# A selective-scan and attention kernel: preparing images 3 and 4 beside attention, taking shared buffers together, and a denser share of products on TensorE

## The chip, the cores and the metric

The kernel runs on one core of a Trainium2 chip. Its engines work side by side, each through its own queue in order: PE (TensorE, matrix products), DVE (VectorE), ACT (ScalarE, activation functions and copies), POOL (GpSimd), and SP (SyncE), which here only issues DMAs. The metric is the device time of one execution in microseconds (us), less is better.

## The reference

Four images of 384 channels and 32x32 positions go through a selective-scan layer, causal attention and a mixture of four experts. Everything is float32. Shortened:

```
x = x + conv(_gn(x), ...)                  # group norm in front
  # conv: xs = the image in 4 directions (rows, columns, both reversed)
  x_dbl = einsum('bkdl,kcd->bkcl', xs, x_proj_weight)   # -> dts (12), Bs (16), Cs (16)
  dt = softplus(einsum('bkrl,kdr->bkdl', dts, dt_projs_weight) + dt_projs_bias)
  def step(h, inp):                        # scan over 1024 positions
      dA = exp(dtt[..., None] * A)
      h = h * dA + (dtt * ut)[..., None] * bt[:, :, None, :]
      y = einsum('bkdn,bkn->bkd', h, ct)
  ys = ys + Ds * u ; merge the 4 directions ; layer norm ; exact gelu
t = tokens(x)                              # 1024 tokens of 384
t = t + attn(_ln_t(t), Wq, Wk, Wv)         # one head of 384, causal softmax
t = t + ffn(_ln_t(t), ...)                 # best 2 of 4 experts kept, 384 -> 1536 -> 384
```

## The kernel before

**Units.** The scan of an image is cut into 192 units, 768 in all. A unit is a tile of 128 partitions (32 channels by 4 states) and 1024 positions. For each unit ACT makes the decay `da` (L552, exp), DVE the input `v` = `du` x B (L559, `front`) and the scan `h` (L565, `middle`), POOL the product `h` x C (L572, `back`), and after every four units PE sums over states into `y` (L597, `row`). `back` of a unit is ordered behind `front` of the next one, so that POOL's product runs beside a scan and not beside a product of DVE. `da` has three buffers, so ACT can be two units ahead at most.

**`v` by PE, image 0 only.** In the first image PE has little else to do. For some groups of four units the side program `feed` lets PE turn `du` (`turn`, L815), ACT scales the turned tile by B (32 small activations per group, L838, into `st`), and PE turns it back into `v` (L860, `turned`), so that DVE doesn't make that product. Before, these are the groups with odd `q`, where time permits.

**Preparation.** `preparation(b)` loads an image, takes the group norm, projects it (`project_x`), and for each of 3 channel blocks and 2 pairs of directions runs `project_dt`: two halves of matmuls `pdt` (L425), softplus on ACT (L431), a DMA of `dt` to memory, the product `du` (L439) on DVE and its DMA. The scan fetches both from memory, a few units ahead. Exp and softplus need different function tables on ACT, so that each change between `da` and `dt` loads a table. One preparation runs at a time; `yield "wait", n` lets n steps pass.

**What follows the scan.** After an image's last unit its sum is evicted (L617), layer-normed and gated (`finish`), and `behind(b)` runs its attention and experts beside the scan of the next image, from the list `waiting`, one image at a time. The last image's run alone after the last unit. In the scores' softmax (L1012 to L1018) DVE takes the minimum of each block, of two blocks at L1016, and ACT the exponential.

**Order of the work.** All of it is written out by hand, by a clock that advances one step per unit. In each step the main loop puts down, in this order: `decay` of two units ahead, deferred work, `front`, `turned`, `back`, inner work such as the softmax, `middle`, `row`, fetches, one piece of the running preparation, and then `go_on`, which steps side programs and the head of `waiting`. `go_on` has a budget of PE time per step, `pace`: PACE_A (4.4) in attention and PACE_E in the experts; each generator says with `yield "pe", n` what it used. Because every engine works in order, a place in this sequence is a place in each queue.

**Shared buffers.** Eight SBUF slots of 4 KB per partition (`slots`) and four PSUM banks (`banks`) are handed out by `Shared`. Expert weights, `dt` and `du` tiles, attention's weights and probabilities and the squares of layer norms all live in slots; `take` waits until one is free, step by step.

Of the kernel before, what the change touches and what calls it, by code (L numbers as in the profile page):

```python
# [9 lines left out]
AF = mybir.ActivationFunctionType  # L10
ALU = mybir.AluOpType
# [4 lines left out]
P = 128  # L16
B = 4
C = 384
M = C // P
HW = 32  # L20
L = HW * HW
# [12 lines left out]
NQ = N // NI  # L34
NJ = P // DJ
# [7 lines left out]
AHEAD = 5  # L43
SLOTS = 8
PACE_A = 4.4
PACE_E = 3.3


@with_exitstack
def hybrid_kernel(  # L50
# [22 lines left out]
    nc = tc.nc  # L73
# [37 lines left out]
    clock = [-100]  # L111
# [6 lines left out]
    class Shared:  # L118
# [15 lines left out]
        def take(self, name, *shape):  # L134
            while not self.ready():
                yield "wait", 1
            return self.now(name, *shape)

        def give(self, *names):
            for name in names:  # L140
# [268 lines left out]
    def project_dt(b, pair, m, u, xd):  # L409

        ks = PAIRS[pair]
        while not slots.ready(3 + pair):
            yield "wait", 1
        v = u[m]
        if pair == 1:
            v = slots.now(f"ut_{b}_{m}", P, L)
            nc.scalar.copy(v.rearrange("p (w h) -> p w h", h=HW), columns(u[m]))
        dts = [slots.now(f"dt_{b}_{k}_{m}", P, L) for k in ks]
        for h in range(NH):
            while not banks.ready(2):  # L420
                yield "wait", 1
            pss = [banks.now(f"pdt_{b}_{k}_{m}_{h}") for k in ks]
            for i, k in enumerate(ks):
                r = slice(64 * pair + 32 * i, 64 * pair + 32 * i + R)
                nc.tensor.matmul(  # L425
                    pss[i], wdt[r, m * P : (m + 1) * P], xd[r, bass.ts(h, 512)],
                    start=True, stop=True,
                )
            yield "wait", 1
            for i, k in enumerate(ks):  # L430
                nc.scalar.activation(  # L431
                    dts[i][:, bass.ts(h, 512)], pss[i], AF.Softplus, bias=dtb[:, k, m : m + 1]
                )
                banks.give(f"pdt_{b}_{k}_{m}_{h}")
        yield "wait", 1
        for i, k in enumerate(ks):
            nc.sync.dma_start(dts_d[b, k][0, m * P : (m + 1) * P, :], dts[i])
            du = yield from slots.take(f"du_{b}_{k}_{m}", P, L)
            nc.vector.tensor_mul(du, dts[i], v)  # L439
            yield "wait", 1  # L440
            nc.sync.dma_start(dts_d[b, k][1, m * P : (m + 1) * P, :], du)
            if b == 0:
                stored_du.add((k, m))
            slots.give(f"dt_{b}_{k}_{m}", f"du_{b}_{k}_{m}")
        if pair == 1:
            slots.give(f"ut_{b}_{m}")

    EACH = NQ * NJ
    IMAGE = M * K * EACH
# [30 lines left out]

    def preparation(b):

        u = first_x if b == 0 else load_image(b)
        yield "wait", 3
        yield from groupnorm(b, u)
        while clock[0] < IMAGE * (b - 1) + 24:

            yield "wait", 1
        xd = one.tile([P, L], F32, tag="xd", name=f"xd_{b}")
        if b == 0:  # L490
            nc.scalar.activation(dump, eps, AF.Softplus)
            scan_weights()
        yield from project_x(b, 0, u, xd)
        if b == 0:
            fetch(-3, ("bc",))
            first_dt(u, xd)
            yield "start", 0
        yield from project_x(b, 1, u, xd)
        for m in range(M):
            for pair in range(2):  # L500
                if b > 0 or m > 0 or pair > 0:
                    yield from project_dt(b, pair, m, u, xd)
                yield "wait", 0 if b == 0 and m == 0 else 12

    units = [
        dict(b=b, pair=pair, i=i, k=k, m=m, q=q, j=j, name=f"{b}_{m}_{k}_{q}_{j}")
# [120 lines left out]
    def layernorm(dst, src, name, lag):  # L627

        width = src.shape[2]
        n = width // 512
        mus = []
        for h in range(n):
            mu = yield from banks.take(f"mu_{name}_{h}")
            for c in range(M):
                nc.tensor.matmul(  # L640
                    mu, mean_w, src[:, c, bass.ts(h, 512)], start=(c == 0), stop=(c == M - 1)
                )
            mus.append(mu)
            yield "pe", 2.6
        yield "inner", 0
        for h in range(n):
            s = bass.ts(h, 512)
            nc.vector.tensor_tensor(
                dst[:, :, s], src[:, :, s], mus[h].unsqueeze(1).to_broadcast([P, M, 512]),
                ALU.subtract,  # L650
            )
            banks.give(f"mu_{name}_{h}")
        sqs = []
        for c in range(M):
            sq = yield from slots.take(f"sq_{name}_{c}", P, width)
            sqs.append(sq)
        for h in range(n):
            for c in range(M):
                s = bass.ts(h, 512)
                nc.scalar.activation(sqs[c][:, s], dst[:, c, s], AF.Square)  # L660
        yield "wait", lag
        var = yield from banks.take(f"var_{name}")
        for h in range(n):
            for c in range(M):
                for q in range(4):
                    o = h * 512 + q * P
                    nc.tensor.matmul(
                        var[32 * q : 32 * (q + 1), h * P : (h + 1) * P], mean_w[:, :32],
                        sqs[c][:, o : o + P], start=(c == 0), stop=(c == M - 1),
                        tile_position=(0, 32 * q),  # L670
                    )
            yield "pe", 1.0
        slots.give(*[f"sq_{name}_{c}" for c in range(M)])
        rs = one.tile([P, n, P], F32, tag=f"rs{n}", name=f"rs_{name}")
        nc.scalar.activation(
            rs, var[:, : n * P].rearrange("p (h t) -> p h t", t=P), AF.Sqrt, bias=eps
        )
        banks.give(f"var_{name}")
        yield "wait", 1
        nc.vector.reciprocal(rs, rs)  # L680
        yield "wait", lag
        backs = []
        for h in range(n):
            spread_ = yield from banks.take(f"rb_{name}_{h}")
            for q in range(4):
                nc.tensor.matmul(  # L686
                    spread_[:, q * P : (q + 1) * P],
                    ident[:, 32 * q : 32 * q + 1].to_broadcast([P, P]), rs[:, h, :],
                    start=True, stop=True,
                )  # L690
# [85 lines left out]
    def feed():  # L776
# [21 lines left out]
        for n in range(0, IMAGE, EACH):  # L798
# [16 lines left out]
                    nc.tensor.transpose(ps[:, t * P : (t + 1) * P], du[:, o : o + P], ident)  # L815
                return ps

            for q in range(1, NQ, 2):
                n0 = n + q * NJ
                if clock[0] > n0 - AHEAD:  # L820
                    continue
                while len(begun) >= 2 and clock[0] < begun[-2] + NJ:

# [61 lines left out]

            defer(1 + m // 2, add)

    def scaled_tokens(b, yb):

        sqs = []  # L890
        for c in range(M):
            sq = yield from slots.take(f"sq_at_{b}_{c}", P, L)
            nc.scalar.activation(sq, yb[:, c, :], AF.Square)
            sqs.append(sq)

        var = yield from banks.take(f"var_at_{b}")
        for o, src in ((NH * P, [yb[:, c, :] for c in range(M)]), (0, sqs)):
# [10 lines left out]
        slots.give(*[f"sq_at_{b}_{c}" for c in range(M)])  # L908
        rs = one.tile([P, NH, P], F32, tag=f"rs{NH}", name=f"rs_at_{b}")
        flat = rs.rearrange("p h t -> p (h t)")  # L910
        nc.scalar.activation(flat, var[:, NH * P : 2 * NH * P], AF.Square)
        yield "inner", 0
        nc.vector.tensor_tensor(flat, var[:, : NH * P], flat, ALU.subtract)
# [28 lines left out]
    def attention(b, yb, fx0):  # L942
# [2 lines left out]
        while not folded:  # L945
            yield "wait", 1
        gw_ = []
        for name, w in ((f"wg_{b}", g_d), (f"wv_{b}", wv_d)):
            ta = yield from slots.take(f"{name}a", P, 2, C)
            nc.sync.dma_start(ta, w[:, :2, :])  # L950
            tb = yield from slots.take(f"{name}b", P, C)
            nc.sync.dma_start(tb, w[:, 2, :])
            gw_.append((ta[:, 0, :], ta[:, 1, :], tb))
        xn = yield from scaled_tokens(b, yb)
        qt = pools["ht"].tile([P, M, L], F32, tag="ht", name=f"qt_{b}")
        vt = pools["ht"].tile([P, L // P, C], F32, tag="ht", name=f"vt_{b}")

# [50 lines left out]
        def softmax(i, ss, pr):  # L1008
# [4 lines left out]
            for n, (o, e, ps) in enumerate(ss):  # L1013
                nc.vector.tensor_reduce(nb[:, n : n + 1], ps, AX.X, ALU.min)  # L1014
            if len(ss) == 2:
                nc.vector.tensor_tensor(nb[:, 0:1], nb[:, 0:1], nb[:, 1:2], ALU.min)  # L1016
            for n, (o, e, ps) in enumerate(ss):
                nc.scalar.activation(  # L1018
                    pr[:, o:e], ps, AF.Exp, bias=nb[:, 0:1], scale=-1.0,
# [5 lines left out]
        def normalise(i, nb, n):  # L1025
            wd = (i + 1) * P
            if n == 2:
                nc.vector.tensor_add(nb[:, 2:3], nb[:, 2:3], nb[:, 3:4])
            nc.vector.reciprocal(nb[:, 2:3], nb[:, 2:3])
            nc.scalar.activation(prs[i][:, :wd], prs[i][:, :wd], AF.Copy, scale=nb[:, 2:3])  # L1030

# [445 lines left out]
```

## Time and profile before

| | us |
|---|---|
| median of 3 runs | 3781.38 (3779.78 to 3781.87) |
| profiled execution | 3782.19 |
| its span | 3780.4 |

```profile
PE 3348.6 (89%) x11755; PEld 1523.6 (40%) x11755; DVE 2962.4 (78%) x2098; ACT 2088.0 (55%) x2754; POOL 1815.4 (48%) x776
...
L565 DVE TENSOR_TENSOR_SCAN h<-da,v 128x1024 f32<-128x1024 f32 x768 | 1750.6, 2284 | 107.2 <-PE v L860 31.8
L552 ACT ACTIVATE da<-dt,a 128x1024 f32<-128x1024 f32 x768 | 882.8, 1156 | 916.0 <-DVE h L565 877.8
L559 DVE TENSOR_TENSOR v<-du,bc 128x1024 f32<-128x1024 f32 x678 | 840.6, 1240 | 35.0 <-DMA du<-dts 18.3
```

The first line gives each engine's busy time, its share of the span and its instructions. In the others stand line, engine, operation, output and inputs, shape and count, then busy us and mean ns of one, then the idle time of the engine just before such instructions and what ended most of it. The shares are averages over stages that differ: image 0 has no attention or experts beside it, and after the last unit there is no scan.

### The profile page before, as it was taken

How to read it: one execution, taken by the hardware profiler on the slowest of the kernel's cores; microseconds unless marked ns; L12 is line 12 of the kernel's file. 1: busy time of each engine (PE TensorE's matmuls, PEld its weight loads, DVE VectorE, ACT ScalarE, POOL GpSimd, SP SyncE). 2: the span in 40 equal slices, each digit the busy share in tenths (PEclk: the TensorE clock that was granted, in tenths of full speed). 3: DMA queues.
4: the chain of work that ended last, by engine and by line, in shares of the span. 5: the costliest groups of instructions: out<-in, count | busy, mean ns of one | idle time of the engine just before them, and what ended most of it. 6: DMA issues, size and time to landing. Idle time of an engine off the chain costs nothing. (4 is left out here: it accounts for less than half of the span.)

```text
span 3780.4 us, 34707 instructions
## 1 busy us (share of the span) xinstructions
PE 3348.6 (89%) x11755; PEld 1523.6 (40%) x11755; DVE 2962.4 (78%) x2098; ACT 2088.0 (55%) x2754; POOL 1815.4 (48%) x776
## 2 busy tenths in 40 slices
PE   4666666689999999799999999889999998999999
PEld 1333323345343334345333344454344334644444
DVE  5899899988899899989988999999999992210000
ACT  5888888555666556556655555455554552322121
POOL 2777777545466556545555565455665660000000
PEclk7777876799999999898999999899999999999999
DMA  6656555635676757436666655455667551322321
GB/s 202 221 211 223 203 210 200 235 141 177 211 247 210 253 197 245 152 136 219 218 218 227 203 201 197 143 172 196 209 197 241 178 182 38 91 78 81 97 82 53
DMA packets 408017, 680.01 MB, mean 180 GB/s; under 512 B 33520, under 2 KB 279968, under 8 KB 407840
## 3 DMA queue, kind: packets, MB, share of 16 engines
q1 hardware_dynamic: 401632, 677.40, 52.6%
q8 instruction: 93, 1.52, 0.2%
q10 hardware_dynamic: 6208, 0.39, 0.1%
q14 instruction: 84, 0.69, 0.1%
HBM read 605.16 MB, written 72.55 MB: 179 GB/s over the span
## 5 line engine op out<-in xcount | busy, mean ns | idle before, releaser
L572 POOL TENSOR_TENSOR h<-h,bc 128x1024 f32<-128x1024 f32 x768 | 1814.3, 2367 | 1300.8 <-DVE v L559 1170.4
L565 DVE TENSOR_TENSOR_SCAN h<-da,v 128x1024 f32<-128x1024 f32 x768 | 1750.6, 2284 | 107.2 <-PE v L860 31.8
L552 ACT ACTIVATE da<-dt,a 128x1024 f32<-128x1024 f32 x768 | 882.8, 1156 | 916.0 <-DVE h L565 877.8
L1260 PE MATMUL ph<-fx,w 128*128 128x512 f32 x2304 | 1023.3, 600 | 3.5 <-DMA w<-in_w 2.0
L1285 PE MATMUL fy<-ht,w 128*128 128x512 f32 x2304 | 1022.4, 601 | 1.7 <-ACT dt L431 0.9
L559 DVE TENSOR_TENSOR v<-du,bc 128x1024 f32<-128x1024 f32 x678 | 840.6, 1240 | 35.0 <-DMA du<-dts 18.3
L1285 PEld LDWEIGHTS fy<-ht,w 128*128 128x128 f32 x2304 | 437.1, 192 | 575.9 <-issue 558.9
L1260 PEld LDWEIGHTS ph<-fx,w 128*128 128x128 f32 x2304 | 433.8, 191 | 578.6 <-issue 532.8
L597 PE MATMUL y<-h,sel 128*32 128x512 f32 x3072 | 489.7, 659 | 97.4 <-POOL h L572 97.2
L1245 ACT ACTIVATE ht<-ph,b1s 128x512 f32<-128x512 f32 x384 | 257.5, 678 | 463.3 <-PE ph L1260 462.5
L1294 DVE SCALAR_TENSOR_TENSOR fy<-fy,b2s,tw 128x512 f32<-128x512 f32 x96 | 72.4, 754 | 423.0 <-PE fy L1285 423.0
L597 PEld LDWEIGHTS y<-h,sel 128*32 128x32 f32 x3072 | 97.6, 116 | 407.4 <-issue 219.0
L860 PE MATMUL v<-ident,st 128*128 128x128 f32 x720 | 144.2, 366 | 112.7 <-DVE h L565 111.6
L838 ACT ACTIVATE st<-turn,bt 128x128 f32<-128x128 f32 x736 | 213.6, 532 | 0.1
L860 PEld LDWEIGHTS v<-ident,st 128*128 128x128 f32 x720 | 116.1, 190 | 158.3 <-DVE h L565 77.9
L1249 ACT ACTIVATE ht<-ht 128x3072 f32<-128x3072 f32 x64 | 176.9, 2764 | 0.8
L552 ACT ACT_TABLE_LOAD x108 | 138.6, 1283 | 15.5 <-DMA dt<-dts 11.8
L1067 PE MATMUL po<-pt,vt 128*128 128x256 f32 x480 | 110.2, 383 | 10.1 <-ACT pt L959 10.0
L425 PE MATMUL pdt<-xd,wdt 12*128 12x512 f32 x184 | 78.9, 753 | 33.4 <-ACT dt L431 24.7
L997 PE MATMUL ss<-axn,qt 128*128 128x512 f32 (+3 forms) x288 | 101.3, 497 | 7.7 <-ACT yb L1084 6.4
L1067 PEld LDWEIGHTS po<-pt,vt 128*128 128x128 f32 x480 | 96.0, 204 | 27.8 <-ACT pt L959 13.1
L997 PEld LDWEIGHTS ss<-axn,qt 128*128 128x128 f32 x288 | 50.5, 193 | 50.2 <-issue 30.0
(208 smaller groups left out, 1618.3 us busy)
## 6 DMA issues: line engine op xcount, KB each, us to landing
bc<-rows SPq DMA_DIRECT2D x384, 512.0 KB, 4.7
w<-in_w SPq DMA_DIRECT2D x384, 384.0 KB, 5.9
dt<-dts SPq DMA_DIRECT2D x192, 512.0 KB, 3.9
du<-dts SPq DMA_DIRECT2D x192, 512.0 KB, 6.5
dts<-dt SPq DMA_DIRECT2D x48, 512.0 KB, 3.6
dts<-du SPq DMA_DIRECT2D x48, 512.0 KB, 3.8
fx<-t2d SPq DMA_DIRECT2D x12, 768.0 KB, 5.8
tw<-mkd SPq DMA_DIRECT2D x32, 256.0 KB, 6.5
```

Source lines behind the costliest of these rows:

```text
L552: nc.scalar.activation(u["da"], spread["dt4", n], AF.Exp, scale=a4[:, g, u["q"] : u["q"] + 1])
L559: return nc.vector.tensor_tensor(u["v"], spread["du4", n], spread["bc", n][:, 0, :], ALU.mult)
L565: nc.vector.tensor_tensor_scan(u["h"][:, ::step], u["da"][:, ::step], u["v"][:, ::step], 0.0, op0=ALU.mult, op1=ALU.add,)
L572: product = nc.gpsimd.tensor_tensor(h, h, spread["bc", n][:, 1, :], ALU.mult)
L597: nc.tensor.matmul(y, sel, h, start=first, stop=last, tile_position=(0, jj * DJ))
L838: nc.scalar.activation(st[:, 4 * h + t, :].rearrange("p (d i) -> p i d", i=NI)[:, i, :], ps[h][:, t * P : (t + 1) * P], AF.Copy, scale=bt[ ...
L860: nc.tensor.transpose(u["v"][:, t * P : (t + 1) * P], st[:, t, u["j"] * P : (u["j"] + 1) * P], ident)
L1067: nc.tensor.matmul(pv[:, o:], vt[:, j, m * P : (m + 1) * P], pts[step][j // 4][:, j % 4, o:], start=(alone and j == 0), stop=(j == nj - 1),)
L1245: nc.scalar.activation(ht[:, f, :], ps, AF.Identity, bias=bias)
L1249: nc.scalar.activation(ht, ht, AF.Gelu)
L1260: nc.tensor.matmul(ps, tiles[n][:, c, (f % 2) * P : (f % 2 + 1) * P], xns[h][:, c, :], start=(c == 0), stop=(c == M - 1),)
L1285: nc.tensor.matmul(pss[m], tiles[n][:, f, :], hts[fh][:, f, :], start=(fh == 0 and f == 0), stop=(fh == 1 and f == FH - 1),)
```

## The change

- `PACE_E` goes from 3.3 to 3.45.
- `together` takes several slots at once when all are free; the squares of the layer norms use it.
- In `project_dt` the wait between the first and the second half's matmuls and activations is left out for the second half as long as the first image is scanned.
- `preparation` of images 2 and 3 (counted from 0) starts at most 30 steps before the image in front of them is scanned, their projections start with that image instead of 24 steps later, and the pauses between projections become 4 steps for image 1 and 1 step for images 2 and 3, where they were 12.
- In `feed` the groups that PE makes are those whose number leaves 1, 3 or 4 when divided by 5, instead of the odd ones.
- Attention fetches its weights into slots after its squares are given back, instead of before.
- Two operations on one number per partition in the softmax are `tensor_scalar` instead of `tensor_tensor`.

```diff
-PACE_E = 3.3
+PACE_E = 3.45
@@ class Shared
+        def together(self, names, *shape):
+            while not self.ready(len(names)):
+                yield "wait", 1
+            return [self.now(name, *shape) for name in names]
@@ project_dt
-            yield "wait", 1
+            if h == 0 or clock[0] >= IMAGE:
+                yield "wait", 1
@@ preparation
+        while b > 1 and clock[0] < IMAGE * (b - 1) - 30:
+            yield "wait", 1
         u = first_x if b == 0 else load_image(b)
...
-        while clock[0] < IMAGE * (b - 1) + 24:
+        while clock[0] < IMAGE * (b - 1):
             yield "wait", 1
...
-                yield "wait", 0 if b == 0 and m == 0 else 12
+                yield "wait", (0 if m == 0 else 12, 4, 1, 1)[b]
@@ layernorm
-        sqs = []
-        for c in range(M):
-            sq = yield from slots.take(f"sq_{name}_{c}", P, width)
-            sqs.append(sq)
+        sqs = yield from slots.together([f"sq_{name}_{c}" for c in range(M)], P, width)
@@ feed
-            for q in range(1, NQ, 2):
+            for q in range(NQ):
                 n0 = n + q * NJ
-                if clock[0] > n0 - AHEAD:
+                if n0 // NJ % 5 not in (1, 3, 4) or clock[0] > n0 - AHEAD:
                     continue
@@ scaled_tokens(b, yb, between)
+        sqs = yield from slots.together([f"sq_at_{b}_{c}" for c in range(M)], P, L)
         for c in range(M):
-            sq = yield from slots.take(f"sq_at_{b}_{c}", P, L)
-            nc.scalar.activation(sq, yb[:, c, :], AF.Square)
-            sqs.append(sq)
+            nc.scalar.activation(sqs[c], yb[:, c, :], AF.Square)
...
         slots.give(*[f"sq_at_{b}_{c}" for c in range(M)])
...
+        while not slots.ready(4):
+            yield "wait", 1
+        between()
@@ attention
-        for name, w in ((f"wg_{b}", g_d), (f"wv_{b}", wv_d)):
-            ta = yield from slots.take(f"{name}a", P, 2, C)
...
-        xn = yield from scaled_tokens(b, yb)
+        def weights():
+            for name, w in ((f"wg_{b}", g_d), (f"wv_{b}", wv_d)):
+                ta = slots.now(f"{name}a", P, 2, C)
...
+        xn = yield from scaled_tokens(b, yb, weights)
@@ scores
-                nc.vector.tensor_tensor(nb[:, 0:1], nb[:, 0:1], nb[:, 1:2], ALU.min)
+                nc.vector.tensor_scalar_min(nb[:, 0:1], nb[:, 0:1], nb[:, 1:2])
@@ normalise
-                nc.vector.tensor_add(nb[:, 2:3], nb[:, 2:3], nb[:, 3:4])
+                nc.vector.tensor_scalar_add(nb[:, 2:3], nb[:, 2:3], nb[:, 3:4])
```

More of the change, by code (lines that the diff above doesn't have):

```diff
@@ L886, in finish, with scaled_tokens @@
             defer(1 + m // 2, add)
-    def scaled_tokens(b, yb):
-        sqs = []
+    def scaled_tokens(b, yb, between):
+        sqs = yield from slots.together([f"sq_at_{b}_{c}" for c in range(M)], P, L)
         for c in range(M):
-            sq = yield from slots.take(f"sq_at_{b}_{c}", P, L)
-            nc.scalar.activation(sq, yb[:, c, :], AF.Square)
-            sqs.append(sq)
+            nc.scalar.activation(sqs[c], yb[:, c, :], AF.Square)
         var = yield from banks.take(f"var_at_{b}")
@@ L947, in attention @@
         gw_ = []
-        for name, w in ((f"wg_{b}", g_d), (f"wv_{b}", wv_d)):
-            ta = yield from slots.take(f"{name}a", P, 2, C)
[L950 to L953, printed above, removed]
-        xn = yield from scaled_tokens(b, yb)
+        def weights():
+            for name, w in ((f"wg_{b}", g_d), (f"wv_{b}", wv_d)):
+                ta = slots.now(f"{name}a", P, 2, C)
+                nc.sync.dma_start(ta, w[:, :2, :])
+                tb = slots.now(f"{name}b", P, C)
+                nc.sync.dma_start(tb, w[:, 2, :])
+                gw_.append((ta[:, 0, :], ta[:, 1, :], tb))
+        xn = yield from scaled_tokens(b, yb, weights)
         qt = pools["ht"].tile([P, M, L], F32, tag="ht", name=f"qt_{b}")
```

## The prediction

> **What bounds the kernel now.** I read the windows first, cut where the scans of units 0, 192, 384, 576 begin (the view of tile `h` gives 50.3, 682.9, 1511.4 and 2331.6), at the end of the last scan (3114.3) and where the last image's projections begin (3177).
>
> ```profile
> core 0: us, PE busy (x) PEld busy (x) DVE busy (x) ACT busy (x) POOL busy (x), PEclk, DMA share, GB/s
> 50.30:682.90 632.60, 394.61 (x1806) 192.61 (x1806) 582.57 (x327) 517.62 (x1047) 454.72 (x191) 0.72 0.61 216
> 682.90:1511.40 828.50, 772.58 (x2781) 347.98 (x2782) 765.08 (x543) 502.41 (x547) 452.55 (x192) 0.96 0.60 210
> 1511.40:2331.60 820.20, 773.59 (x2654) 335.36 (x2653) 762.65 (x526) 470.65 (x496) 452.34 (x192) 0.96 0.58 200
> 2331.60:3114.30 782.70, 743.25 (x2596) 327.10 (x2595) 748.90 (x512) 416.71 (x442) 452.22 (x192) 0.97 0.56 188
> 3114.30:3177.00 62.70, 50.00 (x275) 26.27 (x274) 21.75 (x20) 18.92 (x20) 2.47 (x2) 0.88 0.17 57
> 3177.00:3780.00 603.00, 594.27 (x1590) 284.38 (x1590) 65.88 (x131) 147.99 (x189) 0.00 (x0) 1.00 0.26 76
> ```
>
> The scans set the pace: DVE is busy for 92 to 96% of each of the first four windows. In image 0 ACT is next (82%), in the other images PE (93 to 95%). After 3177 PE alone matters; the chain of waits runs there through `ph` and `fy` with no gaps, so nothing in the change can shorten those 603 us. What DVE waits for in images 1 to 3, and in image 0:
>
> ```profile
> DVE nb L1014 <- PE ss L1002: 22.6, 6, 10.8
> DVE du L439 <- PE ph L1260: 16.8, 3, 10.0
> DVE du L439 <- PE fy L1285: 13.9, 4, 7.7
> ...
> DVE du L439 <- ACT dt L431: 3.3, 3, 1.9
> ...
> DVE h L565 <- PE v L860: 31.8, 22, 3.8
> ```
>
> The `du` product of a preparation waits for its delta projection, which stands in PE's queue behind expert matmuls: 35 us with the smaller rows (1.0 for `da`), 19 of them in image 1, 16 in image 2. The last line is image 0's: nearly every group of four whose `v` PE makes ends in a wait of about 1.45 us.
>
> One row is out of proportion, a minimum over two numbers per partition:
>
> ```profile
> L1016 DVE TENSOR_TENSOR nb<-nb x16: 159/1303/1712, 825.8 to 3242.5; 128x1 f32<-128x1 f32 x16
> 862.47 2.34 POOL L572 TENSOR_TENSOR h<-h,bc 128x1024 f32<-128x1024 f32 x1 [1.86 <-DVE v L559]
> 863.53 1.30 DVE L1016 TENSOR_TENSOR nb<-nb 128x1 f32<-128x1 f32 x1
> 864.75 2.27 DVE L565 TENSOR_TENSOR_SCAN h<-da,v 128x1024 f32<-128x1024 f32 x1
> L341 DVE TENSOR_SCALAR gn_vc<-gn_vc x3: 154/155/155, 358.7 to 1407.5; 128x3 f32<-128x3 f32 x3
> ```
>
> It starts inside POOL's product (862.47 to 864.81) and ends with it. In the last image, with POOL silent, it takes 0.16.
>
> Where the scans end, experts of image 2 are still in PE's queue and hold up the last image:
>
> ```profile
> 3112.04 2.29 DVE L565 TENSOR_TENSOR_SCAN h<-da,v 128x1024 f32<-128x1024 f32 x1
> 3125.65 1.28 DVE L617 SCALAR_TENSOR_TENSOR yb<-xe,dsum,y 128x1024 f32<-128x1024 f32 x1 [11.32 <-PE y L597]
> 3133.54 1.75 DVE L648 TENSOR_TENSOR yb<-yb,mu_l 128x1536 f32<-128x1536 f32 x1 [6.61 <-PE mu_l L640]
> ```
>
> [...] 1.30 us beside POOL, 0.16 without. [...] For three elements the trace shows no such wait (0.155 us at L341, 0.23 at L340, POOL running); for one element no run here shows it. [...] a load from 1017.79 is followed by its softplus at 1019.08. I price a switch at 1.28.
>
> **The change part by part.**
>
> *Minimum by `tensor_scalar`.* 12 of the 16 minima lie among scans, at 1.37 us mean, four per image from 1 to 3. At 0.16 to 0.24 each, 4 x 1.2 = 5 us per image, on DVE and just ahead of a scan. Bounds: 0 [...] and 15 in all. The adds at L1028 take 0.13 already: nothing.
>
> *Which groups PE makes (`q` loop).* The orders of both programs give 208 instead of 184 transposes into `turn` and 824 instead of 720 into `v`, that is 103 units instead of 90. DVE loses 13 products of 1.24 plus a 0.06 gap: -17 us. Two more `du` fall into image 0 (those that image 1 has after unit 192 now): +2.6. In the new pattern two such groups often stand in a row. ACT gets 96 more scalings at 0.30 (8 took 2.42): +28; and as both halves of a projection are now activated together before unit 192, 11 pairs of table loads go: -28. Two more projections and the third image's statistics also enter: +20. So ACT has about 537 us of work for some 620, and the projections of image 1, spread over units 110 to 204 before, now stand at 105 to 159, where ACT's work comes to 3.2 to 3.3 us a unit against DVE's 3.0 to 3.4. I take 1.45 us of wait for each of the three further groups and 3 us for that crowding: -14.4 + 7.3 = -7. Bounds: -20 (waits go with the table loads) and +8 (ACT sets the pace in units 96 to 168).
>
> *Preparations beside attention.* Image 2's projections move from units 238 to 335 to units 192 to 233, image 3's from 408 to 504 to 384 to 426; their 2 x 12 `du` stay, and so do their PE and ACT work and their DMAs (12 loads of `x` and stores of `xn`, rows and dts: their data are needed 150 units later). The `du` waits among experts go: -19 and -16. In the new place they stand behind PE's `pq` and `pv`, where DVE already waits 5.3 and 10.8 us (`nb` L1014), and ACT gets about 8.7 us per projection (half a 1.98 copy, four 0.65 softplus, four loads of 1.28). Counted from the changed program's order with the durations of before, ACT comes to 3.3 to 4.4 us per unit there, DVE to 4.4 to 5.1, so DVE still leads on the average; in-order queues will cost something: I take +8 per image. Bounds 0 and +30. Image 1 also loses 2 `du` (-2.6).
>
> *`together`, and weights fetched after the squares (`between`).* Same allocations and DMAs, other moments. SP's landing time for such transfers is 4 to 7 us and three more steps of attention follow before `pq`: 0, covered by the normalisation; if not, under 7 us per image.
>
> *PACE_E 3.45.* An expert counts 12 x 2.6 + 6 x 5.1 = 61.8: 18.7 units before, 17.9 after. PE needs 144 x 0.427 = 61.5 us for it plus about 0.48 us of `y` per unit (16 matmuls, 1.92 us, every fourth unit): 70.5 before, 70.1 after. DVE at 3.62 a unit (scan, product, gaps) plus three times 1.44 for `fy`: 72 before, 69.5 after. PE becomes the bound by about 0.6 us per expert: +3 in image 1, +1 in image 2 (its preparation is gone from there), +5 in image 3, where also 2 to 3 more `fy` pairs come in front of the last scan (+3).
> In return image 2's experts end at step 769 instead of 779 of the kernel's clock (its scheduling rules followed through); the last scan is 767. Before, from the scan's end to `pq` are 62.7 us. Without experts in between: POOL 2.4, `y` 1.9, a PE lag of 3, eviction 1.3, means 5.3, subtraction 1.8, squares 1.7, variance 1.5, root and reciprocal 2.2, spreading and product 5: about 26 to the end of L696; from there to `pq` the trace has 20.2 (3156.75 to 3177). 46 to 49 instead of 62.7: -14. Bounds -18 and -4 (PE lags by a whole expert).
>
> Sum: image 0 -7; image 1: -5 - 2.6 - 19 + 8 + 3 = -15; image 2: -5 - 16 + 8 + 1 = -12; image 3: -5 + 3 + 5 = +3; tail -14. Together -45. The profiled execution took 3782.2 (span 3780.4 and 1.8 around it), 0.8 above the median of 3781.4: 3737.
>
> **The rivals.** *All waits go* (attention takes the projections for nothing, image 0 keeps its full 14): -45 - 16 - 7 = -68, with lower waits at L860 about -78: 3704. For it: DVE leads in every stage by the sums. Against: PE and ACT work in order and would be busy for 80 to 97%. *Attention gives most of it back:* the du waits reappear there at some 3 us each projection more: 3772. For it: those 10.8 us waits at L1014. *Slower: a moved wait.* The 12 projections meet `pq`, `pv` and the softmax in PE's and ACT's queues, and each `du` holds every scan behind it. The two worst such waits now are 7.7 and 10.0; at 8 us for each projection the attention parts lose 96 instead of the 16 I allow: -45 + 80 = +35, 3817. It decides the sign from 5 us per projection on. Against it: PE is busy only 180.5 of 219.3 us in 682.9 to 902.2, while the waits now come from stretches where it is full. *The change doesn't take hold:* minima still blocked (+15) and PE late among experts (+15 more): 3767.
>
> **How the numbers follow.** Forecast (3720 to 3757) 0.60, all waits go 0.14, given back or not taking hold 0.16, slower 0.10. The range, 3702 to 3772, takes in all but the slower case and the ends of the others. Faster than the 0.2% (7.6 us) that a measurement can tell from no change: 0.86, within it 0.04, slower 0.10.
>
> **What would show it.** L1026 (the minimum) at 0.2 us; no `du` waits behind `ph` or `fy`, and below 25 us behind others; 103 units by PE and image 0 near 625 us; `nb` waits of 30 us or less; 46 to 50 us from the last scan to `pq`; PE at 97% among experts. It is wrong if image 0 is longer than 633, if attention stretches lengthen by over 30 us each beyond their added `du`, or if expert units take over 4.0 us.

## The result and the profile after

| | before | after |
|---|---|---|
| median of 8 runs each, us | 3781.28 (3779.78 to 3784.8) | 3769.9 (3768.69 to 3772.26) |
| ratio | | 0.9968 (0.9959 to 0.9978) |
| span of the profiled execution | 3780.4 | 3770.5 |

The change makes the kernel 11.4 us faster, a quarter of the 44 forecast. The page of the changed kernel, with the engines' line, the scan and the product `v`:

```profile
PE 3354.8 (89%) x11883; PEld 1539.0 (41%) x11883; DVE 2951.9 (78%) x2085; ACT 2084.8 (55%) x2832; POOL 1817.5 (48%) x776
...
L574 DVE TENSOR_TENSOR_SCAN h<-da,v 128x1024 f32<-128x1024 f32 x768 | 1749.7, 2284 | 110.7 <-PE v L866 19.9
L568 DVE TENSOR_TENSOR v<-du,bc 128x1024 f32<-128x1024 f32 x665 | 825.2, 1241 | 40.0 <-DMA du<-dts 20.9
```

The count of `v` fell by the 13 forecast (678 to 665), its time by 15.4 us, and yet DVE's whole busy time fell by only 10.5. The windows of the changed kernel say where; the cuts are again the scans of units 0, 192, 384 and 576, and the last scan's end:

```profile
core 0: us, PE busy (x) PEld busy (x) DVE busy (x) ACT busy (x) POOL busy (x), PEclk, DMA share, GB/s
47.90:693.40 645.50, 419.10 (x1972) 207.85 (x1972) 587.23 (x327) 530.89 (x1148) 455.30 (x191) 0.74 0.61 222
693.40:1501.40 808.00, 759.61 (x2741) 342.35 (x2742) 756.77 (x531) 483.14 (x522) 452.88 (x192) 0.96 0.60 206
1501.40:2324.80 823.40, 770.49 (x2653) 340.84 (x2652) 759.92 (x526) 472.85 (x496) 452.93 (x192) 0.95 0.58 199
2324.80:3114.00 789.20, 755.08 (x2640) 334.04 (x2639) 745.87 (x514) 421.24 (x443) 452.94 (x192) 0.97 0.56 188
3114.00:3770.50 656.50, 631.52 (x1822) 304.48 (x1821) 86.59 (x148) 162.94 (x207) 2.35 (x1) 0.98 0.25 75
```

Since the scans on DVE carry the first four windows, each difference splits into DVE's work and DVE's idle time (length less busy time). Against the windows of before, and against the terms of the prediction:

| window | measured: work | idle | sum | forecast: work | idle | sum |
|---|---|---|---|---|---|---|
| image 0 | +4.7 | +8.2 | +12.9 | -14.4 | +7.3 | -7 |
| image 1 | -8.3 | -12.2 | -20.5 | -7.6 | -8 | -15.6 |
| image 2 | -2.7 | +5.9 | +3.2 | -5 | -7 | -12 |
| image 3 | -3.0 | +9.5 | +6.5 | -2 | +5 | +3 |
| after the last scan | | | -9.6 | | | -14 |
| ahead of the first scan | | | -2.4 | | | 0 |

In image 3 the forecast's further `fy` pairs (+3) are counted as work. Two entries carry the miss of 35: the work in image 0 (19 us more than forecast) and the idle time in image 2 (13 more). What the rows of image 0 show in the changed kernel, by groups (out and inputs, count, busy us and mean ns, idle before):

```profile
L568 DVE TENSOR_TENSOR v<-du,bc 128x1024 f32<-128x1024 f32 x89 | 115.1, 1293 | 7.4 <-DMA du<-dts 6.2 <-DMA bc<-rows 1.0
L446 DVE TENSOR_TENSOR du<-dt,ut 128x1024 f32<-128x1024 f32 x12 | 18.9, 1573 | 5.8 <-ACT dt L438 5.8
L446 DVE TENSOR_TENSOR du<-dt,x 128x1024 f32<-128x1024 f32 x10 | 16.0, 1601 | 4.0 <-ACT dt L438 4.0
```

In the kernel before, the same two products took 1.25 and 1.27 us each and waited for nothing:

```profile
L439 DVE TENSOR_TENSOR du<-dt,x 128x1024 f32<-128x1024 f32 x10 | 12.7, 1272 | 0.0
L439 DVE TENSOR_TENSOR du<-dt,ut 128x1024 f32<-128x1024 f32 x10 | 12.5, 1248 | 0.0
```

So `v` gave 14.8 us (129.9 to 115.1), while `du` cost 9.7 more (25.2 to 34.9) and the `gn` operations of the group norms 9.4 more (1.6 to 11.0). The timeline of the changed kernel shows what happens to one pair of `du` (start, us, engine, line and operation, idle before):

```profile
512.44 1.27 ACT L438 ACTIVATE dt<-pdt,dtb 128x512 f32<-128x512 f32 x2 [1.58 <-PE pdt L430]
512.86 2.35 POOL L581 TENSOR_TENSOR h<-h,bc 128x1024 f32<-128x1024 f32 x1 [2.47 <-DVE h L574]
513.16 3.13 DVE L446 TENSOR_TENSOR du<-dt,ut 128x1024 f32<-128x1024 f32 x1 [0.39 <-ACT dt L438]
...
518.41 1.19 DVE L446 TENSOR_TENSOR du<-dt,ut 128x1024 f32<-128x1024 f32 x1
518.57 3.26 POOL L581 TENSOR_TENSOR h<-h,bc 128x1024 f32<-128x1024 f32 x1 [3.36 <-DVE h L574]
```

The first `du` waits 0.39 us for the first of ACT's two softplus of that pair, starts 0.30 us into POOL's product, and ends 1.08 us after it (516.29 against 515.21): it was held until POOL's product ended. All 12 `du` of image 0 that start inside a product of POOL end 1.08 to 1.10 us after it, whether 0.10 or 2.29 us of it were left, and take 1.20 to 3.37 us. The second `du` of the pair starts 0.16 us ahead of POOL's product, and now POOL's takes 3.26 us, where it took 2.35 above. So it went both ways round here: what started first took its usual time, and the other ended late. An operation on three elements was held in the same way: the three long ones below (2.38, 1.35 and 2.30 us) each end 0.02 us after a product of POOL. The tile `gn_dev` of the changed kernel in image 0 (shortest, median and longest of the two, ns):

```profile
L364 DVE TENSOR_TENSOR gn_dev<-gn_mc,gn_mean x2: 1352/1866/2381, 354.8 to 641.8; 128x3 f32<-128x3 f32 x2
L365 DVE TENSOR_TENSOR gn_dev<-gn_dev x2: 161/1232/2303, 357.2 to 643.2; 128x3 f32<-128x3 f32 x2
```

In image 2 the new idle time lies in the 54 units that have attention and the six moved projections, with their twelve `du`, beside them (1501.4 to 1776.7): 38.8 us, where the same units had 20.2 before, a rise of 18.5 before rounding. The waits in that stretch (us, times, longest); `ss` are attention's scores and `nb` the minima of their softmax, `yb` is the image that has just been scanned, `y` the sum over its states and `mu_l` the means of its layer norm:

```profile
DVE nb L1024 <- PE ss L1012: 11.4, 3, 5.9
DVE du L446 <- ACT dt L438: 8.2, 1, 8.2
DVE yb L657 <- PE mu_l L649: 6.7, 1, 6.7
DVE yb L626 <- PE y L606: 4.6, 1, 4.6
```

Before, the first of these was 12.0 and the others were not there: the three new ones, 19.5 us together, account for the rise. PE's queue in the changed kernel shows what stands ahead of `y` and `mu_l` (start, us):

```profile
1507.09 2.74 PE L397 MATMUL pxd<-x,wx 128*128 128x512 f32 x6
1514.91 1.92 PE L606 MATMUL y<-h,sel 128*32 128x512 f32 x16
...
1527.17 2.74 PE L649 MATMUL mu_l<-yb,mean_w 128*128 128x512 f32 x6
1529.74 2.74 PE L397 MATMUL pxd<-x,wx 128*128 128x512 f32 x6
...
1539.42 2.84 PE L649 MATMUL mu_l<-yb,mean_w 128*128 128x512 f32 x6
```

`pxd` is `project_x` of the preparation that was moved here, four blocks of 2.74 to 2.84 us between 1507 and 1532.5, among the last matmuls of the preceding image's experts. Before, those experts stood there too, but no `pxd`: the 12 matmuls of `mu_l` ran as one block, and DVE waited for neither. Among the experts that follow, idle time fell from 37.3 to 24.7 us: the `du` waits went, as forecast.

The end went as forecast. The windows of the changed kernel from the last scan's end to the last image's first `pq`, and from there on:

```profile
3114.00:3163.75 49.75, 34.10 (x232) 19.02 (x231) 20.29 (x18) 14.90 (x18) 2.35 (x1) 0.80 0.22 71
3163.75:3770.50 606.75, 597.42 (x1590) 285.46 (x1590) 66.31 (x131) 148.04 (x189) 0.00 (x0) 0.99 0.26 75
```

62.7 us became 49.75. Against that stand 3.3 us that the same 1590 matmuls took longer, which leaves the -9.6; over the traces of this study they took between 601.2 and 606.9 us. The four images repeat better: where the code of an image agrees, its traces lie within 3 us of each other (image 0 in six traces 642.8 to 645.5, image 2 in three 823.3 to 825.0). Smaller differences of a stage are not read below, and a run's median and its profiled execution may differ by up to 7 us.

### The profile page after: what moved, and what is told of

It is laid out like the page before. It is cut to its first block, busy times and chain, and to the rows that moved or that the text cites. A ratio compares the mean times of both kernels' runs of the same rounds, so it can differ in the third digit from the quotient of the medians.

```text
span 3770.5 us, 35085 instructions
## 1 busy us (share of the span) xinstructions
PE 3354.8 (89%) x11883; PEld 1539.0 (41%) x11883; DVE 2951.9 (78%) x2085; ACT 2084.8 (55%) x2832; POOL 1817.5 (48%) x776
## 4 chain that ended last, share of the span: by engine, by line
PE 70%; DVE 17%; ACT 5%; issue 4%; DMA 3%; POOL 1%; SPq 0%; DVEq 0%; POOLq 0%; ACTq 0%
PE ph L1270 25%; PE fy L1295 25%; DVE h L574 9%; PE y L606 7%; DVE v L568 5%; PE ss L1007 2%; PE pq L978 2%; ACT st L844 2%; PE pv L989 2%; PE po L1077 1%; ACT da L561 1%; PE pxd L397 1%; PE v L866 1%; DVE du L446 1%; PE pdt L430 1%
## 5 line engine op out<-in xcount | busy, mean ns | idle before, releaser
L574 DVE TENSOR_TENSOR_SCAN h<-da,v 128x1024 f32<-128x1024 f32 x768 | 1749.7, 2284 | 110.7 <-PE v L866 19.9
L1270 PE MATMUL ph<-fx,w 128*128 128x512 f32 x2304 | 1017.9, 598 | 10.5 <-DMA w<-in_w 9.6
L568 DVE TENSOR_TENSOR v<-du,bc 128x1024 f32<-128x1024 f32 x665 | 825.2, 1241 | 40.0 <-DMA du<-dts 20.9
L606 PE MATMUL y<-h,sel 128*32 128x512 f32 x3072 | 470.0, 653 | 90.7 <-POOL h L581 88.8
L844 ACT ACTIVATE st<-turn,bt 128x128 f32<-128x128 f32 x832 | 244.7, 558 | 0.8 <-PE turn L821 0.7
L430 PE MATMUL pdt<-xd,wdt 12*128 12x512 f32 x184 | 89.7, 804 | 43.0 <-ACT dt L438 16.3
L1007 PE MATMUL ss<-axn,qt 128*128 128x512 f32 (+3 forms) x288 | 113.6, 544 | 7.7 <-ACT yb L1094 4.1
```

Source lines behind the costliest of these rows:

```text
L568: return nc.vector.tensor_tensor(u["v"], spread["du4", n], spread["bc", n][:, 0, :], ALU.mult)
L574: nc.vector.tensor_tensor_scan(u["h"][:, ::step], u["da"][:, ::step], u["v"][:, ::step], 0.0, op0=ALU.mult, op1=ALU.add,)
L606: nc.tensor.matmul(y, sel, h, start=first, stop=last, tile_position=(0, jj * DJ))
L844: nc.scalar.activation(st[:, 4 * h + t, :].rearrange("p (d i) -> p i d", i=NI)[:, i, :], ps[h][:, t * P : (t + 1) * P], AF.Copy, scale=bt[ ...
L1007: nc.tensor.matmul(ps[:, : e - o], qt[:, c, i * P : (i + 1) * P], xn[:, c, o:e], start=(c == 0), stop=(c == M - 1 and (alone or e <= i * P)),)
L1270: nc.tensor.matmul(ps, tiles[n][:, c, (f % 2) * P : (f % 2 + 1) * P], xns[h][:, c, :], start=(c == 0), stop=(c == M - 1),)
```

## The experiments

Ratios are to the kernel before, with 95% intervals; the changed kernel is at 0.9968. Stages are of one trace each. All but the last two are the changed kernel with one part undone or altered, or several.

**The old pattern of groups made by PE** (u1_groups).

```diff
-            for q in range(NQ):
+            for q in range(1, NQ, 2):
                 n0 = n + q * NJ
-                if n0 // NJ % 5 not in (1, 3, 4) or clock[0] > n0 - AHEAD:
+                if clock[0] > n0 - AHEAD:
```

> The changed kernel with the old choice of groups for PE (odd ones, 23 instead of 26). Image 0 (first scan to the scan of unit 192) took 632.6 us before and 645.5 us changed, against 626 forecast. If it is the pattern of groups (two in a row) that costs image 0 its time, it is back at 630 to 635 here and the whole at about 3757. If it is the joined halves (du products that wait for softplus, 9.8 us, and by that fall into POOL's products), image 0 stays at 642 to 650, with du waits of 7 us or more.

3779.33 us, 0.999 (0.9983 to 0.9997). Image 0 took 648.9 us, with 100 `v` products by DVE, `du` still at 1.44 us, though with `du` waits of 3.5 us only, and `gn` operations at 5.3 us in sum. The denser pattern is therefore not what lengthened image 0; by the medians it is worth some 9 us, of which this one trace shows 3.4 in image 0.

**The wait between a projection's halves put back** (u2_halves).

```diff
-            if h == 0 or clock[0] >= IMAGE:
-                yield "wait", 1
+            yield "wait", 1
```

> The changed kernel with the step between the two halves of a projection put back in image 0. If the joined halves are the cause, the du waits for softplus (9.8 us) go, du products take 1.25 to 1.35 us on the mean instead of 1.59, and image 0 comes to 628 to 635 although ACT has 11 more pairs of table loads (28 us). If ACT's load is the cause, image 0 gets longer: 650 us or more. If it is the pattern of groups, it stays at 642 to 648.

3779.86 us, 0.9991 (0.9985 to 0.9998): a miss on the time. The `du` waits were gone and `du` took 1.24 us, which the theory asked for, but image 0 took 651.1 us. With softplus spread out again, the scaled tiles of 12 units came too late to be turned (ACT made 832 scalings, as in the changed kernel, PE only 728 instead of 824 transposes into `v`), and DVE had to make these products itself. The row `v` of image 0 in this kernel has 101, not 89:

```profile
L566 DVE TENSOR_TENSOR v<-du,bc 128x1024 f32<-128x1024 f32 x101 | 129.9, 1286 | 8.3 <-DMA du<-dts 6.0 <-DMA bc<-rows 2.2
```

So this run takes away two things at once. ACT was busy for 553.5 instead of 530.9 us, and 651.1 us also fits what was expected if ACT's load were the cause; this run can't tell the two apart. The next keeps the halves together and ACT's load near that of the changed kernel (523.4 us).

**`du` one step later in image 0** (u3_du_later).

```diff
                 banks.give(f"pdt_{b}_{k}_{m}_{h}")
-        yield "wait", 1
+        yield "wait", 2 if clock[0] < IMAGE else 1
```

> The changed kernel with joined halves kept, and the du products put down one step later in image 0. If du is only too early behind its softplus[...]: image 0 at 625 to 633. If ACT's load or the pattern is the cause, it stays at 642 to 648.

3763.79 us, 0.9952 (0.9937 to 0.9967). Image 0 took 636.7 us, 8.8 less, though not the 625 to 633 expected. By groups, the two `du` rows of image 0 in this kernel:

```profile
L446 DVE TENSOR_TENSOR du<-dt,ut 128x1024 f32<-128x1024 f32 x12 | 15.6, 1303 | 0.0
L446 DVE TENSOR_TENSOR du<-dt,x 128x1024 f32<-128x1024 f32 x10 | 12.1, 1212 | 0.0
```

34.9 us of `du` became 27.7, the waits of 9.8 us are gone, and `v` stays at 88 products. The waits of scans for PE's `v` rose from 19.9 to 40.1 us, so not all of it is kept. Image 1 took 815.1 us, 7.0 more than in the changed kernel: the preparation beside image 0 ends later, and the projections of the next one start some 8 units later.

**The group norm's small operands in PSUM** (u4_gn_psum). The deviation and the root stay in the PSUM tile of their matmul, so that each product has one input outside SBUF:

```diff
-        nc.vector.tensor_sub(dev, mean_c, mean)
-        nc.vector.tensor_mul(dev, dev, dev)
-        nc.vector.tensor_add(dev, dev, var_c)
+        nc.vector.tensor_sub(dev, mean_c, ps)
+        nc.vector.tensor_sub(ps, mean_c, ps)
+        nc.vector.tensor_mul(ps, dev, ps)
+        nc.vector.tensor_add(dev, ps, var_c)
...
-        nc.vector.scalar_tensor_tensor(mean, mean, -1.0, rstd, ALU.mult, ALU.mult)
+        nc.vector.reciprocal(ps, ps)
+        nc.vector.scalar_tensor_tensor(mean, mean, -1.0, ps, ALU.mult, ALU.mult)
```

> The changed kernel with the group norm's small products (two SBUF inputs each) reading one of their inputs from PSUM. In the changed kernel four of them took 1.35 to 2.38 us beside POOL's products, 8.4 us together instead of 0.64. [...] each takes 0.2 us or less here, and image 0 loses up to 7 us: 637 to 641. If they only stand where DVE would have waited anyway, they become short and image 0 stays at 644 to 646.

3765.09 us, 0.9953 (0.9938 to 0.9968). The `gn` operations of image 0 went from 11.0 to 3.9 us, and image 0 from 645.5 to 637.5. The tile `gn_dev` of this kernel has the same subtraction and square:

```profile
L363 DVE TENSOR_TENSOR gn_dev<-gn_mc,gn_mean x2: 135/140/146, 356.3 to 640.4; 128x3 f32<-128x3 f32 x2
L365 DVE TENSOR_TENSOR gn_mean<-gn_dev,gn_mean x2: 166/166/167, 356.6 to 640.7; 128x3 f32<-128x3 f32 x2
```

Up to 2.38 us became 0.14, and 2.30 became 0.17, although POOL ran through both pairs (the second at 640.41 and 640.65, POOL's products from 639.09 to 646.13): the wait for POOL's product, not the operation or its place, was the cost, and with one input in PSUM it was gone.

**Image 3's projections 12 steps later** (u5_late3).

```diff
-        while clock[0] < IMAGE * (b - 1):
+        while clock[0] < IMAGE * (b - 1) + (12 if b == 3 else 0):
```

> The changed kernel with the projections of image 3 started 12 steps later, after the experts of image 1 have left PE's queue. Image 2 took 820.2 us before and 823.3 changed, against 808 forecast. If the overlap with those experts is the cause (waits of 4.6 for y and 6.7 for the means behind unit 384), both waits go and image 2 comes to 808 to 813. If the collision with attention itself is the cause, image 2 stays at 820 or more, with the du and softmax waits (8.2 and 12.0 us) as long or longer.

3764.36 us, 0.9954 (0.9939 to 0.9969). The 54 units took 267.5 instead of 275.3 us. The waits for `mu_l` and for ACT's `dt` left this stretch and that for `y` fell from 4.6 to 2.0 us, with `mu_l` in one block on PE again; so it is the `pxd` among those experts that made them. But two waits of 7.8 us in sum for the means of the experts' norm came in, `ss` stayed at 11.1, and image 2 as a whole fell by 4.0 us only, short of what was expected. Most of what this move wins comes back as other waits.

**The old pace among experts** (u6_pace).

```diff
-PACE_E = 3.45
+PACE_E = 3.3
```

> The changed kernel with PACE_E back at 3.3. If the higher pace makes PE late in image 3 (789.2 us, 782.7 before) and shortens the end (656.5, 666.1 before), image 3 falls to 781 to 785 and the end grows to 668 or more, as experts of image 2 now end at step 786; the whole at 3775 to 3785. If image 3's extra time has another source, image 3 stays at 787 or more.

3775.71 us, 0.9986 (0.9978 to 0.9994). Image 3 took 7.5 us less (781.7) and the part after the last scan 18.4 more (674.9), while the way to `pq` took 24.0 more (73.8 instead of 49.75). Images 1 and 2 took 5.2 and 3.1 us less as well, so the higher pace costs something in three images. It is a trade, worth about 6 us by the medians.

**The minimum as `tensor_tensor`** (u7_min_tt).

```diff
-                nc.vector.tensor_scalar_min(nb[:, 0:1], nb[:, 0:1], nb[:, 1:2])
+                nc.vector.tensor_tensor(nb[:, 0:1], nb[:, 0:1], nb[:, 1:2], ALU.min)
```

> The changed kernel with the minimum over two numbers as tensor_tensor again. [...] the 12 minima among scans take 0.7 to 1.7 us again instead of about 0.2, images 1 to 3 grow by 3 to 5 us each, the whole by 10 to 15. If DVE would have waited there anyway, the minima are long and the images grow by less than 2 us each.

3777.1 us, 0.9988 (0.9981 to 0.9995), 7.2 above the changed kernel, where 10 to 15 were expected. Images 1 to 3 took 2.8, 3.3 and 3.6 us longer, and DVE's busy time in them rose by 9.0: the edit is worth some 10 of the forecast 15 us. The same row here and in the changed kernel:

```profile
L1026 DVE TENSOR_TENSOR nb<-nb x16: 158/471/1716, 853.6 to 3237.4; 128x1 f32<-128x1 f32 x16
L1026 DVE TENSOR_SCALAR nb<-nb x16: 212/214/215, 855.1 to 3229.1; 128x1 f32<-128x1 f32 x16
```

In both kernels eight of the 16 start inside a product of POOL. As `tensor_tensor` these eight take 0.78 to 1.72 us and end within 0.02 us of POOL's end; the other eight take 0.16. As `tensor_scalar` all take 0.21, and most of the eight end well before POOL does. In the kernel before, 12 started inside a product of POOL; four now stand elsewhere, which is why the edit is worth less than forecast.

**The preparations of images 2 and 3 where they were before** (u8_prep_spread).

```diff
-        while b > 1 and clock[0] < IMAGE * (b - 1) - 30:
+        while b > 1 and clock[0] < IMAGE * (b - 1) + 24:
...
-        while clock[0] < IMAGE * (b - 1):
+        while clock[0] < IMAGE * (b - 1) + (24 if b > 1 else 0):
...
-                yield "wait", (0 if m == 0 else 12, 4, 1, 1)[b]
+                yield "wait", (0 if m == 0 else 12, 4, 12, 12)[b]
```

> The changed kernel with the preparations of images 2 and 3 spread over the experts again, as before the change (start 24 steps into the image in front, pauses of 12). If moving them beside attention paid in both images, images 1 and 2 take 820 us or more and 835 or more here, against 808 and 823. If PE has too much work wherever the preparation stands, image 2 stays at 818 to 828 and only the place of the waits changes.

3770.95 us, 0.9974 (0.9962 to 0.9985): the changed kernel's time. Image 0 took 10.4 us less, images 1 and 2 only 3.4 and 4.9 more, both short of what was expected if the move pays:

```profile
48.60:683.70 635.10, 413.41 (x1942) 206.51 (x1942) 579.66 (x316) 519.18 (x1130) 455.21 (x191) 0.73 0.61 221
683.70:1495.10 811.40, 769.71 (x2777) 344.49 (x2777) 756.02 (x532) 491.22 (x528) 452.75 (x193) 0.97 0.60 207
1495.10:2323.40 828.30, 783.59 (x2699) 339.64 (x2698) 761.62 (x538) 483.51 (x513) 453.95 (x193) 0.96 0.60 203
```

Without the third image's statistics in image 0 its `gn` operations took 3.6 us instead of 11.0. The `du` waits among experts were back (9.6 us in image 1, 13.5 in image 2), and the 54 units of image 2 took 250.1 instead of 275.3 us, with 22.6 instead of 38.8 us of idle time on DVE. So the moved preparation is what made the idle time there, and the move, as made, is worth nothing: 8 us won in images 1 and 2 against 10 lost in image 0.

**Du later, operands in PSUM and image 3 later together** (u11_combo; the edits of u3, u4 and u5).

> The changed kernel with du one step later in image 0, the group norm's small products through PSUM, and the projections of image 3 started 12 steps later. If the three causes are separate and add up, image 0 takes 627 to 632, image 2 808 to 814, and the whole 3740 to 3750. If they share one wait, the whole stays above 3755.

3757.44 us, 0.9935 (0.9918 to 0.9951). Image 0 took 627.2 us with DVE busy 569.1, inside the 627 to 632 expected if the causes are separate; the whole missed its 3740 to 3750, since images 1 and 2 took 814.1 and 819.8 us, not less. Image 1 is as long as in u3, whose edit is in here.

**The same with image 1's pauses at 3** (u12_combo).

```diff
-                yield "wait", (0 if m == 0 else 12, 4, 1, 1)[b]
+                yield "wait", (0 if m == 0 else 12, 3, 1, 1)[b]
```

> The four things together: du one step later in image 0, group norm's small products through PSUM, image 3's projections 12 steps later, and pauses of 3 instead of 4 in image 1's preparation, so that image 2's starts at unit 192 again (it slipped to 197 in the combination before, where image 1 took 814.1). Image 0 at 627 to 633, image 1 at 805 to 810, image 2 at 818 to 821, the whole 3745 to 3754.

3755.85 us, 0.9931 (0.9918 to 0.9945), just outside what was expected, and with u11, from which noise does not part it, the fastest version that computes everything: 25 us under the kernel before and 14 under the changed one. Image 1 came back to 808.7 us and image 0 went to 634.2, where scans waited 39.8 us for PE's `v`.

**A third of `ph` left out in images 0 to 2** (n1_light_experts): `for c in range(2)` instead of 3 there. `ph` is an expert's first layer. This kernel and the next compute less than they should; they tell of times only.

> The changed kernel with one of the three matmuls of every first expert layer left out for images 0 to 2 (82 us of PE per image less, everything else in the same order). If PE's amount of work is what holds DVE among the experts, the waits for y and the means (4.6, 6.7 and scans behind y) go and images 1, 2 and 3 take 795 or less, 808 or less and 782 or less, while the 20 us of softmax and du waits in the attention part of image 2 stay. If it is latency between engines, no image gets shorter by more than 5 us.

3751.61 us in a single run. Images 1 to 3 took 4.3, 8.3 and 5.8 us less, not the 13, 15 and 7 expected. In the 54 units of image 2 `ss` (11.9) and `du` (9.7) stayed; only `y` and `mu_l` shrank. Taking 82 us of PE's work out of each image's experts thus wins 4 to 8 us.

**A third of `pq`, `pv` and `ss` left out in images 0 to 2** (n2_light_attn): the same edit at these three matmul loops, attention's projections and scores.

> The changed kernel with one of the three matmuls left out in attention's q and v projections and scores for images 0 to 2 (about 18 us of PE per image less). If the softmax and du waits beside attention are PE's backlog, the stretch of units 384 to 438 (275 us) gets shorter by 8 to 18 us and these waits (12.0 and 8.2) fall below 10 together. If they come from ACT's queue or from the length of the chain, the stretch changes by less than 4 us.

3740.46 us in a single run. Images 1 to 3 took 10.0, 10.9 and 8.7 us less. The 54 units took 264.7 us instead of 275.3, with DVE's busy time unchanged (236.5). Their waits:

```profile
DVE nb L1025 <- PE ss L1013: 7.1, 3, 3.6
DVE yb L657 <- PE mu_l L649: 6.7, 1, 6.7
...
DVE nb L1025 <- PE ss L1008: 0.9, 1, 0.9
DVE du L446 <- ACT dt L438: 0.6, 1, 0.6
```

`ss` and `du` together went from 20.1 to 8.6 us, `mu_l` and `y` stayed. Although the releaser of the `du` wait is written as ACT, less work on PE took it away. The changed kernel shows the way (PE, ACT and DVE, in order of time):

```profile
1645.28 1.76 PE L430 MATMUL pdt<-xd,wdt 12*128 12x512 f32 x4
1645.39 0.48 ACT L969 COPY vt<-pv 128x384 f32<-128x384 f32 x1 [1.46 <-PE pv L989]
1647.18 1.27 ACT L438 ACTIVATE dt<-pdt,dtb 128x512 f32<-128x512 f32 x2
...
1652.09 0.48 ACT L969 COPY vt<-pv 128x384 f32<-128x384 f32 x1 [0.82 <-PE pv L989]
1653.88 1.27 ACT L438 ACTIVATE dt<-pdt,dtb 128x512 f32<-128x512 f32 x2
1654.60 1.23 DVE L446 TENSOR_TENSOR du<-dt,ut 128x1024 f32<-128x1024 f32 x1 [8.22 <-ACT dt L438]
```

The second half's `pdt` is done at 1647.04, 6.8 us before its softplus starts: it is not `pdt` that is late. The softplus stands in ACT's queue behind the copies `vt` of attention's values, table loads and a decay; the copies wait for attention's `pv` on PE, and `du` waits behind the softplus.

## Where the prediction held and why it failed

The time, 3769.9, lies inside the range of 3702 to 3772 only because the range took in the rivals too; the gain is a quarter of the forecast, and image 0, at 645.5 us, is longer than the 633 that the prediction itself named as a sign of being wrong.

*Right in mechanism and size.* The 13 products that PE takes over (-14.8, forecast -16 without its gaps), the minima's cost per operation (1.37 to 0.21 us), the `du` waits among experts, and the way from the last scan to `pq` (49.75, forecast 46 to 49). Image 1 did 5 us better than forecast: its `du` and `ss` waits beside attention came to 12.5 us, where such waits were 5.3 before, so that the +8 allowed held there.

*The first failed step: "DVE loses 13 products ... -17 us. Two more `du` fall into image 0 ...: +2.6 ... Two more projections and the third image's statistics also enter: +20" (on ACT).* It priced all 22 `du` at the 1.25 us of before and the statistics' DVE operations at nothing. The prediction had read the wait for POOL at one row, the minimum, and priced it there alone, though `du` and the small `gn` operations have two SBUF inputs as well and were short before (1.26 us and 0.16) only by where they stood: of POOL's products in which some of them started, at most 0.30 us were left. Bringing the halves together made `dt` late, so that `du` met POOL's product (+7.1 us over its price, and 9.8 us of waits), and the third image's statistics came among POOL's products (+9.4). u3 and u4 each take one away and win 8.8 and 8.0 us in image 0; with both, u11's image 0 has 569.1 us of DVE work, 13.5 under before, where the prediction had 14.4, and takes 627.2 against 632.6, where it had -7. The idle time, +8.2 for a forecast +7.3, was right by luck: scans waited 11.9 us less for PE's `v`, where 4.4 more had been forecast, and the 9.8 us of `du` and further waits for DMAs filled the gap.

*The second: "in-order queues will cost something: I take +8 per image".* In image 2 the idle time beside attention rose by 18.5 us, and u8 shows that the moved preparation makes it. The new waits are 8.2 us for `du`, 6.7 for `mu_l` and 4.6 for `y`; those for `ss` were there before (12.7 us, now 11.9). The `du` wait goes with attention's PE work (n2: 0.6 us). Those for `mu_l` and `y` go, or fall to 2.0, when `project_x` starts 12 steps later (u5); that its matmuls would come ahead of the finished image's sum and means is a term that the prediction put at nothing. The averages that it read (DVE over ACT in every unit) could not show either: the cost is three waits, each holding every scan behind it. Why others come in their place in u5 stays open.

*The smaller ones.* The minima are worth 10, not 15 us, as only eight of the 12 start inside POOL's products in the new order (u7). The denser groups are worth about 9 us net by the medians. Image 3's idle time behind PE rose by 9.5 us, where +5 was forecast, and u6 puts 7.5 us of image 3 on the pace. Here a sum was off: 17.9 units at 3.62 us and 4.3 for `fy` make 69.2 us, not 69.5, so that PE leads by 0.9 and not 0.6 us for each of the image's eight passes through an expert, 7 us and not 5 in all; and the trace of before has 0.429 us from one of these matmuls to the next, not 0.427, which makes it 1.2 us and 10 in all.

*A reading that fails: "For three elements the trace shows no such wait".* The three operations at L340 of the kernel before start some 0.2 us ahead of the end of a POOL product and end 0.02 to 0.03 us after it, so that their 0.23 us could not tell; the last section has one that was held.

*The rivals.* "Given back" was the nearest in time (3772) and half right in cause; the moved wait exists, at 8.2 us once and 5.2 once, not twelve times. That all waits go is refuted by image 2.

## What to carry to other kernels

When an edit moves a DVE operation with two SBUF inputs, as `du`, the minimum and the `gn` operations are here, or puts a new one in, look at what POOL is doing at its new place, and price it at its own time plus what is left of POOL's product (`du` took up to 3.37 us instead of 1.19), even if it works on three elements (2.38 instead of 0.16). The scan was an exception here (at most 2.29 us in 217 places inside POOL's products). An operand in PSUM avoided the wait for the small operations of u4 (0.14 to 0.17 us), and a `tensor_scalar` form for one element per partition (0.21), but not for three (0.45). When a chain across engines (PE, ACT, DVE) is moved beside other work, price it by the queue ahead of each of its links, also by what its first link puts in front of others, not by the mean load per unit. And cut the changed profile into stages, each split into the bounding engine's work and its idle time: a small total here was the sum of -20 and +13.

## What the runs showed that was not expected

- An operation on two three-element tiles took up to 2.38 us beside POOL and 0.14 to 0.17 with one input in PSUM. A one-element `tensor_scalar` took 0.21 in all 16 places, eight of them inside a product of POOL, but one on three elements took longer there. In the changed kernel's row below, the longest starts 0.43 us ahead of POOL's end and ends 0.02 after it; the other two start with POOL idle:

```profile
L345 DVE TENSOR_SCALAR gn_mc<-gn_mc x3: 168/168/448, 340.0 to 1421.1; 128x3 f32<-128x3 f32 x3
```

- The scan, also with both inputs in SBUF, and POOL's product did not hold each other here. In the changed kernel 217 scans start inside a product of POOL and take at most 2.29 us, like the others, and 584 products start inside a scan and take 2.34 to 2.41. The timeline of the changed kernel in image 3 has POOL's product starting 0.04 us into a scan, and both take what they take elsewhere, where `du` and POOL's product above did not; the `v` product, which starts 0.07 us ahead of POOL's end, takes 1.23:

```profile
3001.89 2.29 DVE L574 TENSOR_TENSOR_SCAN h<-da,v 128x1024 f32<-128x1024 f32 x1
3001.93 2.35 POOL L581 TENSOR_TENSOR h<-h,bc 128x1024 f32<-128x1024 f32 x1 [1.34 <-DVE v L568]
3004.21 1.23 DVE L568 TENSOR_TENSOR v<-du,bc 128x1024 f32<-128x1024 f32 x1
```

- The same 1590 matmuls at the end, with almost no waits, took 601.2 to 606.9 us from trace to trace.
